# Layer 0 of a four-layer graph kernel: one mask instruction a tile, loads a step earlier, late sums added a step later

## The chip, the core and the metric

The kernel runs on one core of one Trainium2 chip. The time is the device time of one execution in microseconds; for the kernel before, three executions gave 3460.62, 3468.68 and 3473.94 us, so the median is 3468.68 us. The profile is of one more execution, which took 3465.43 us.

The engines are named as in the profile: PE is the matrix engine (PEld its weight loads), DVE the vector engine, ACT the scalar engine, POOL the GpSimd engine, and SP the engine that in this kernel only issues transfers.

## The reference, cut to what matters

There are 64 graphs of 256 nodes with 256 features (`x`), and a weighted adjacency matrix for each (`adj`). Four layers follow each other, each with a residual and a layer norm. The change is in layer 0, a recurrence over the nodes in which node i reads the states of all nodes:

```python
n = h_e.shape[1]
d = jnp.sum(adj, axis=-1)
dinv = jnp.where(d != 0, 1.0 / jnp.where(d != 0, d, 1.0), 0.0)
norm_adjT = jnp.swapaxes(adj, 1, 2) * dinv[:, :, None]

def step(h, i):
    x = jnp.take(h_e, i, axis=1)
    row = jnp.take(norm_adjT, i, axis=1)
    x_par = jnp.einsum('bj,bjd->bd', row, h)
    iou = x @ W_ioux.T + b_ioux + x_par @ W_iouh.T + b_iouh
    r, z = jnp.split(iou, 2, axis=1)
    r, z = (jax.nn.sigmoid(r), jax.nn.sigmoid(z))
    hc = jnp.tanh(x @ W_coux.T + b_coux + x_par * r @ W_couh.T + b_couh)
    h_new = z * x_par + (1.0 - z) * hc
    h = jax.lax.dynamic_update_slice(h, h_new[:, None, :], (0, i, 0))
    return (h, None)
```

At step i the nodes j < i hold new states, and the nodes j >= i still hold their inputs. Layers 1 to 3 (a graph convolution, a masked attention of one head and one of eight) come afterwards and are the same in both kernels.

## The kernel before, in words

**The two halves of the program.** `_recurrence` is layer 0: 256 steps, one after the other, with all 64 graphs in each step. `_layers` then works through layers 1 to 3 graph by graph. In the trace the first step of the recurrence begins at about 138 us and the last one ends at about 1551 us; the rest of the 3463.7 us belongs to the layers.

**A step.** Step n flips `xp` on PE (`xpT_ps`, L614), copies the result on ACT (L616), multiplies it by the gate weights on PE (L607), and takes the sigmoids on ACT (L830 to L835). DVE forms `rx` (L832), PE flips and multiplies it, ACT takes the tanh (L864), and DVE forms `zcc` (L866) and the next `xp` (L869). That last one needs `v` (L855), which needs `ready` (L806): POOL's scaled copy of the sum for the next node. The order on every engine is written out by hand (`manual_schedule`), and an engine that waits holds up all that is behind it.

**Where the sum of a node comes from.** Steps go in 32 parts of 8 (U = 8). In this text, step 13.6 is the one with p = 6 of part 13. `sums[a]` (`ACC`) holds the sums of the eight nodes of part a, and it is filled from five sides.

- The input side, for nodes j >= i: `Us`, made ahead and loaded by `sums_in` (L315). Its first half is made before the recurrence. The second half is made inside it by `x_side` in pieces of four graphs: 16 tiles `xA` and `xX`. Before use, each `xA` must be masked to its lower triangle on POOL by `cut` (L332). A tile needs four pairs of matrix products (L212, called "products" below), and the kernel before masks it in two halves of two graphs each.
- Newest states: DVE adds them one node at a time (`push`, L632).
- States a few steps old: POOL adds two to four nodes at once (`push_far`, L665 and L669). Early in a part it also does the next part's nodes.
- Late side, for states of about the last 64 steps: `late` (L523) runs on PE in steps p = 0 to 3 and reads the ring `Hw`. ACT copies its results, SP sends them to `Lb` in step p = 3 (L503) and receives them as `late_sb` in step p = 4 (L509). POOL adds `late_sb` to the next part's `ACC` in two halves (L878): in the kernel before, nodes 4 to 7 at the end of step p = 5 and nodes 0 to 3 at the end of step p = 6.
- Early side, for older states: `early_fill` (L420) multiplies tiles `Hs` (states, read back from DRAM) and `A`. The results are stored in `Es` (L432), loaded as `early_sb` (L449) and added on POOL (L819).

**What fills the gaps.** In steps p = 4 to 7 there are two places in each step where PE does early work, if its tiles have been begun at least three steps before (`landed`), or otherwise products of `x_side`: one product a place in p = 4 and 5, two in p = 6 and 7.

**The queue of SP.** All transfers of the recurrence are issued by SP in program order. `into_ring` (L658) writes the states into `Hw`, four transfers in each of the steps p = 4 to 7; `late` of the next part reads them. Loads of `x_side`, of the early side, of `raw` and `S` are put in a list by `load_later` and are begun by `next_load` (L268), two in each of the steps p = 0 to 3. Rows of `adj` for the degrees (L300), `xq` (L571) and the stores are issued where they stand. Every transfer on SP also waits until the one that used its semaphore eight transfers before it has landed.

Of the kernel before, what the change touches and what calls it, by code (L numbers as in the profile page):

```python
# [19 lines left out]
P = 128  # L20
# [50 lines left out]
def _recurrence(tc, ident, Hd, x, adj, W_ioux, b_ioux, W_iouh, b_iouh, W_coux, b_coux, W_couh, b_couh, wide, then):  # L71
# [19 lines left out]
    nc = tc.nc  # L91
# [7 lines left out]
    XB = 4  # L99
# [4 lines left out]
    with ExitStack() as ctx:  # L104
# [7 lines left out]
        tri = const.tile([P, P], F32, name="tri")  # L112
# [96 lines left out]
        def x_product(pb, at, A, Xs):  # L209

            for jc, (a, xs) in enumerate(zip(A, Xs)):
                nc.tensor.matmul(  # L212
                    pb[:, at, :], a, xs, start=(jc == 0), stop=(jc == len(A) - 1)
                )

        def x_out(half, b, ub):

            for c in range(2):
                nc.sync.dma_start(
                    Us[c, b:b + 4, half * P:(half + 1) * P, :].rearrange("b i f -> i b f"),  # L220
                    ub[:, :, c * P:(c + 1) * P],
                )
# [22 lines left out]
        def next_of(queue, n):  # L245
            if queue:
                queue.pop(0)(n)

        def next_load(n):
            if loads:  # L250
                loads.pop(0)[1](n)

        def copy_later(out, in_, then=None):
            def f(n):
                nc.scalar.copy(out, in_)
                held.pop(0)
                if then:
                    then(n)

            copies.append(f)  # L260

        def load_later(out, in_, rank):

            begun = []

            def f(n):
                with nc.allow_non_contiguous_dma(reason="bias vector across partitions"):
                    nc.sync.dma_start(out, in_)  # L268
                begun.append(n)

            loads.append((rank, f))
            loads.sort(key=lambda e: e[0])
            return begun

        def landed(begun, n):

            return all(f and n > f[0] + 2 for f in begun)

        def at_step(n, f):
            transfers.setdefault(n, []).append(f)  # L280
# [3 lines left out]
        def base_bank(shape, name):  # L284

            while len(held) == 3:
                next_of(copies, now)
            held.append(name)
            return ps.tile(shape, F32, tag="base", name=name, bufs=3)
# [31 lines left out]
        def x_side():  # L321

            def load(g):
                A = stream.tile([P, XB, P], F32, tag="xA", name=f"xA2_{g}", bufs=3)
                Xs = stream.tile([P, XB, D], F32, tag="xX", name=f"xX2_{g}", bufs=3)
                return A, Xs, [
                    load_later(to, of.rearrange("b j d -> j b d"), 2)
                    for to, of in ((A, adj[g:g + XB, P:N, P:N]), (Xs, x[g:g + XB, P:N, :]))
                ]

            def cut(A, lo):
                nc.gpsimd.tensor_mul(  # L332
                    A[:, lo:lo + 2], A[:, lo:lo + 2], tri.unsqueeze(1).to_broadcast([P, 2, P])
                )

            tiles = [load(e * XB) for e in range(3)]
            ahead = False
            n = yield
            for g in range(0, B, XB):
                A, Xs, last = tiles.pop(0)  # L340
                while not ahead:
                    if landed(last, n):
                        cut(A, 0)
                        ahead = True
                    n = yield
                ub = stream.tile([P, 4, D], F32, tag="ub", name=f"xu2_{g}")
                for b in range(0, XB, 2):
                    pb = base_bank([P, 2, D], f"xp2_{g}_{b}")
                    for q in range(2):
                        x_product(pb, q, [A[:, b + q, :]], [Xs[:, b + q, :]])  # L350
                        if q:
                            copy_later(ub[:, b:b + 2, :], pb, None if b + 2 < XB else (
                                lambda n, b=g, ub=ub: at_step(n + 1, lambda: x_out(1, b, ub))
                            ))
                            if b + 2 < XB:
                                cut(A, b + 2)
                            else:
                                ahead = bool(tiles) and landed(tiles[0][2], n)
                                if ahead:
                                    cut(tiles[0][0], 0)  # L360
                                if g + 3 * XB < B:
                                    tiles.append(load(g + 3 * XB))
                        n = yield
# [309 lines left out]
        sides = {}  # L673
# [8 lines left out]
        with tc.tile_pool(name="r_first_ps", bufs=4, space=bass.MemoryType.PSUM) as xps:  # L682
            for g in range(0, B, GB):
                A, Xs = first_in.pop(0)
# [3 lines left out]
                for n in range(0, GB, 4):  # L688
                    ub = fst.tile([P, 4, D], F32, tag="ub", name=f"xu_{g}_{n}")
                    for e in range(0, 4, 2):  # L690
                        pb = xps.tile([P, 2, D], F32, tag="x", name=f"xp_{g}_{n}_{e}")
                        for q in range(2):
                            b = n + e + q
# [45 lines left out]
        late_side = background = None  # L739
        behind = []  # L740
        x_left = x_side()
        next(x_left)

# [16 lines left out]
        for now in range(N):  # L760
            n = now
            k, i = divmod(n, T)
            p = n % U
# [104 lines left out]
                xp = new("xp", n + 1)  # L868
                nc.vector.scalar_tensor_tensor(xp, zcc, Sd, v, ALU.mult, ALU.add)  # L869
            next_of(copies, n)  # L870
            if p < 4:
                for _ in range(2):
                    next_load(n)

            if p in (5, 6) and n + 8 - p in sides:
                half = slice(0, U // 2) if p == 6 else slice(U // 2, U)
                part = sums[n // U + 1][:, half]
                nc.gpsimd.tensor_add(part, part, sides[n + 8 - p][:, half])  # L878
# [532 lines left out]
def kernel(ctx: ExitStack, tc: tile.TileContext, ins, out):  # L1411
# [14 lines left out]
    def load_layers(load):  # L1426
        weights.extend(
            _load_layers(nc, wide, load, ins["L1_gnn_W"], ins["L1_gnn_b"], l2, l3)
        )

    _recurrence(
        tc, ident, Hd, x, adj,
        *(ins["L0_gnn_" + n] for n in (
# [44 lines left out]
```

## Time and profile before

| | |
|---|---|
| median of three runs | 3468.68 us (3460.62 to 3473.94) |
| profiled execution | 3465.43 us, span of its instructions 3463.7 us |
| granted PE clock, mean over the span | 0.979 |
| busy: PE, PEld, DVE, ACT, POOL | 93%, 67%, 72%, 54%, 54% of the span |
| recurrence, first to last `xpT_ps` | 137.8 to 1549.1 us |
| mask of `xA` on POOL, 128x256 (L332) | 32 times, 725 ns each |
| addition of `late_sb` on POOL, 128x512 (L878) | 60 times, 1268 ns each |
| transfers | 347.89 MB |

Busy shares are means over the recurrence and the layers, which have different limits, so the recurrence is read from its own stretch. A wait is listed as "who waited <- for whom: total us, times, longest us". In the timeline a line is "start us, duration us, engine, line, operation, out<-in"; the brackets at its end tell how long the engine sat idle before it and what ended that. The length of a step is the distance between the starts of two `xpT_ps` flips (L614) in the timeline of PE. In an undisturbed part the eight steps take 5.30, 5.15, 5.15, 5.28, 5.37, 5.14, 4.88 and 4.88 us, together about 41.2 us (part 28, for one).

### The profile page before, as it was taken

What the parts mean: (1) busy time and instruction counts of PE and PEld (TensorE: products, weight loads), DVE (VectorE), ACT (ScalarE), POOL (GpSimd) and SP (SyncE); (2) the same over time, 40 slices, a digit from 0 to 9 for tenths busy, and PEclk for the clock granted to TensorE, in tenths of its full rate; (3) what the DMA queues carried; (4) which work ended last, traced back from release to release, by engine and by line L of the source; (5) the groups of instructions that cost most, each with busy time, mean ns of one, the idle gap of its engine ahead of it and who ended that gap; (6) DMA issues with size and microseconds to landing.
All of it is one profiled execution on the core that took longest, in us unless ns stands there. A gap on an engine that the chain in (4) does not pass through costs nothing.

```text
span 3463.7 us, 80374 instructions
## 1 busy us (share of the span) xinstructions
PE 3228.6 (93%) x29350; PEld 2320.4 (67%) x29350; DVE 2502.0 (72%) x7061; ACT 1883.4 (54%) x5010; POOL 1873.9 (54%) x2181
## 2 busy tenths in 40 slices
PE   5699999999889898887999999999999999999997
PEld 4555555555555555556888888888888888888885
DVE  3366767766666777754888888888888888888875
ACT  0255545444444454444666666666666666666664
POOL 2366677766566777743444444444444444444443
PEclk8999999999999999997999999999999999999999
DMA  9756576687787575321111111111111111111100
GB/s 301 221 153 143 161 173 154 160 187 187 188 208 168 143 175 145 97 64 54 47 47 47 47 47 46 47 47 46 47 47 47 47 47 47 47 47 47 47 28 19
DMA packets 389348, 347.89 MB, mean 100 GB/s; under 512 B 107356, under 2 KB 355304, under 8 KB 383720
## 3 DMA queue, kind: packets, MB, share of 16 engines
q1 hardware_dynamic: 371256, 325.82, 35.0%
q10 hardware_dynamic: 17696, 16.91, 1.5%
q8 instruction: 235, 3.85, 0.5%
q14 instruction: 161, 1.32, 0.1%
HBM read 224.01 MB, written 99.61 MB: 93 GB/s over the span
## 4 chain that ended last, share of the span: by engine, by line
PE 73%; DVE 7%; DMA 7%; POOL 5%; issue 3%; ACT 2%; SPq 2%; ACTq 0%; DVEq 0%; POOLq 0%
PE mm L999 13%; PE rc L607 5%; PE s L1183 4%; PE rc L599 4%; PE mm_2f L999 4%; PE mm_3v L999 3%; PE mm_t L999 3%; PE mm_3f L999 3%; PE mm_2v L999 3%; PE mm_g L999 3%; PE mm_2s L999 3%; DVE ACC L632 3%; PE o L1218 3%; PE mm_2w L999 3%; PE late L523 3%
## 5 line engine op out<-in xcount | busy, mean ns | idle before, releaser
L632 DVE SCALAR_TENSOR_TENSOR ACC<-keep,S,ACC 128x128 f32<-128x128 f32 x1712 | 503.8, 344 | 186.6 <-ACT hs L650 170.7
L1195 POOL TENSOR_TENSOR p3s<-p 128x256 f32<-128x256 f32 x512 | 387.0, 787 | 366.6 <-ACT p L1193 366.2
L999 PE MATMUL mm<-xT,weights 128*128 128x256 f32 x2048 | 481.9, 383 | 2.9 <-ACT xT L1081 2.9
L999 PEld LDWEIGHTS mm<-xT,weights 128*128 128x128 f32 x2048 | 384.8, 190 | 79.5 <-issue 25.5
L1192 DVE TENSOR_TENSOR p<-s,neg 128x512 f32<-128x512 f32 x512 | 317.5, 682 | 114.5 <-PE s L1183 114.5
L669 POOL TENSOR_TENSOR ACC<-ACC,far 128x384 f32<-128x384 f32 (+1 forms) x313 | 372.3, 1189 | 24.5
L599 PE MATMUL rc<-WxT,xqT 128*64 128x256 f32 x2048 | 326.6, 397 | 4.0 <-ACT rc L840 1.2
L665 POOL TENSOR_TENSOR far<-hs,S 128x384 f32<-128x384 f32 (+1 forms) x313 | 304.3, 972 | 4.7
L963 ACT ACTIVATE y<-y,shift,rstd 128x256 f32<-128x256 f32 x512 | 273.4, 599 | 48.6 <-DVE shift L961 44.7
L806 POOL TENSOR_TENSOR ready<-ACC,dinv 128x128 f32<-128x128 f32 x255 | 101.9, 400 | 364.3 <-DVE ACC L632 363.8
L1193 ACT ACTIVATE p<-p 128x512 f32<-128x512 f32 x512 | 295.0, 628 | 2.1 <-DVE p L1192 1.6
L1106 ACT ACTIVATE qk<-mm,weights 128x256 f32<-128x256 f32 x256 | 107.5, 471 | 268.0 <-PE mm L999 268.0
L1095 POOL TENSOR_TENSOR y<-y,g 128x512 f32<-128x512 f32 x64 | 81.0, 1265 | 267.4 <-issue 267.4
L1232 DVE RECIPROCAL rT<-o 128x256 f32<-128x256 f32 x128 | 223.7, 1748 | 0.2 <-PE o L1209 0.2
L955 POOL TENSOR_TENSOR rstd<-rstd,mhalf 128x2 f32<-128x2 f32 x256 | 173.6, 696 | 84.2 <-DVE rstd L954 82.4
L951 DVE BATCH_NORM_STATS2 st<-y 128x6 f32<-128x256 f32 x512 | 208.8, 408 | 13.4 <-POOL y L1095 12.6
L616 ACT COPY xpT<-xpT_ps 128x128 f32<-128x128 f32 x256 | 68.4, 267 | 265.6 <-PE xpT_ps L614 265.6
L607 PE MATMUL rc<-WhT,xpT 128*64 128x128 f32 x2048 | 170.5, 288 | 28.2 <-ACT xpT L616 28.0
L1060 POOL TENSOR_TENSOR dis<-dis,mhalf 128x2 f32<-128x2 f32 x64 | 44.8, 700 | 277.0 <-DVE dis L1059 252.1
L607 PEld LDWEIGHTS rc<-WhT,xpT 128*64 128x64 f32 x2048 | 107.9, 137 | 118.4 <-ACT xpT L616 84.0
L212 PE MATMUL xp<-xX,xA 128*128 128x256 f32 x384 | 109.4, 423 | 66.3 <-POOL xA L685 39.5
L1158 ACT ACTIVATE qk<-mm,weights 128x256 f32<-128x256 f32 x256 | 107.5, 471 | 115.9 <-PE mm L999 115.9
(162 smaller groups left out, 7485.1 us busy)
## 6 DMA issues: line engine op xcount, KB each, us to landing
xX<-in_x_dram ACTq DMA_DIRECT2D x16, 1024.0 KB
Us<-xu SPq DMA_DIRECT2D x64, 256.0 KB
xq<-in_x_dram SPq DMA_DIRECT2D x64, 256.0 KB
ACC<-Us SPq DMA_DIRECT2D x32, 512.0 KB
Es<-eu SPq DMA_DIRECT2D x64, 256.0 KB
early_sb<-Es SPq DMA_DIRECT2D x32, 512.0 KB
xin<-in_x_dram SPq DMA_DIRECT2D x64, 256.0 KB
ad<-in_adj_dram SPq DMA_DIRECT2D x64, 256.0 KB
```

The costliest lines, as they stand in the source:

```text
L599: nc.tensor.matmul(G[o * B:(o + 1) * B], xqT[a, i // 2][:, i % 2, kc, h * B:(h + 1) * B], WxT[:, kc, o, gates], start=False, stop=False, s ...
L607: nc.tensor.matmul(G[o * B:(o + 1) * B], hT[:, kc * B:(kc + 1) * B], WhT[:, kc, o, g], start=False, stop=(kc == 1), skip_group_check=True,)
L632: nc.vector.scalar_tensor_tensor(acc[:, 0, :], keep[:, j % 2, :], s, acc[:, 0, :], ALU.mult, ALU.add)
L665: nc.gpsimd.tensor_mul(tmp[:, 0:count, :], hs.unsqueeze(1).to_broadcast(shape), s.unsqueeze(2).to_broadcast(shape),)
L669: nc.gpsimd.tensor_add(acc, acc, tmp[:, 0:count, :])
L951: nc.vector.bn_stats(st, y[:, c, :])
L963: nc.scalar.activation(y[:, c, :], y[:, c, :], AF.Identity, bias=shift[:, c:c + 1], scale=rstd[:, c:c + 1],)
L999: nc.tensor.matmul(pm[:, c, :], lhsT[:, k, c * P:(c + 1) * P], rhs[:, k, :], start=(k == 0), stop=(k == 1),)
L1192: nc.vector.tensor_add(p, s_ps[i], self.neg3)
L1193: nc.scalar.activation(p, p, AF.Exp, scale=ISQ)
L1195: nc.gpsimd.tensor_add(both, p[:, 0, :], p[:, 1, :])
L1232: nc.vector.reciprocal(rT, o_ps[:, 1, :])
```

## The change

It makes three edits. The mask of an `xA` tile becomes one POOL instruction over all four graphs (128x512) instead of two over two graphs each. It is still issued when the tile before is finished, or, where the tile's transfers had not been begun three steps before, at the next place. The list of loads is worked off two at a time in steps p = 7, 0, 1 and 2 instead of 0, 1, 2 and 3. The two halves of `late_sb` are added at the end of steps p = 6 (nodes 0 to 3, as before) and p = 7 (nodes 4 to 7, before: p = 5).

```diff
-            def cut(A, lo):
-                nc.gpsimd.tensor_mul(
-                    A[:, lo:lo + 2], A[:, lo:lo + 2], tri.unsqueeze(1).to_broadcast([P, 2, P])
-                )
+            def cut(A):
+                nc.gpsimd.tensor_mul(A, A, tri.unsqueeze(1).to_broadcast([P, XB, P]))
...
                     if landed(last, n):
-                        cut(A, 0)
+                        cut(A)
                         ahead = True
...
-                            if b + 2 < XB:
-                                cut(A, b + 2)
-                            else:
+                            if b + 2 == XB:
                                 ahead = bool(tiles) and landed(tiles[0][2], n)
                                 if ahead:
-                                    cut(tiles[0][0], 0)
+                                    cut(tiles[0][0])
...
-            if p < 4:
+            if p in (7, 0, 1, 2):
                 for _ in range(2):
                     next_load(n)

-            if p in (5, 6) and n + 8 - p in sides:
+            if p in (6, 7) and n + 8 - p in sides:
                 half = slice(0, U // 2) if p == 6 else slice(U // 2, U)
                 part = sums[n // U + 1][:, half]
                 nc.gpsimd.tensor_add(part, part, sides[n + 8 - p][:, half])
```

## The prediction

> **What bounds the kernel now.** I read the lengths of the 256 steps first, from the starts of the `xpT_ps` flips. The 255 distances sum to 1411 us; 31 undisturbed parts of 41.2 us and seven steps of 4.88 would take 1311. So about 100 us are stalls, nearly all in steps p = 6 and 7 of two groups of parts: 30 us in parts 0 to 9 and about 38 us in parts 13 to 19. The lists of waits of POOL and of PE, over 137 to 1551 us, name both:
>
> ```profile
> POOL ready L806 <- DVE ACC L632: 363.8, 201, 6.8
> POOL ACC L878 <- DMA late_sb<-Lb: 44.5, 10, 9.2
> ```
>
> ```profile
> PE xp L212 <- POOL xA L332: 16.8, 15, 2.4
> PE late L523 <- DMA Hw<-hs: 3.5, 1, 3.5
> ```
>
> The first group is PE waiting for a mask. The timelines of POOL and then of PE show it in steps 1.6 and 1.7 (starts 214.06 and 221.37):
>
> ```profile
> 213.34 1.27 POOL L878 TENSOR_TENSOR ACC<-ACC,late_sb 128x512 f32<-128x512 f32 x1
> 214.57 0.72 POOL L332 TENSOR_TENSOR xA<-xA,tri 128x256 f32<-128x256 f32 x1
> 215.38 0.40 POOL L806 TENSOR_TENSOR ready<-ACC,dinv 128x128 f32<-128x128 f32 x1
> 215.74 0.83 POOL L665 TENSOR_TENSOR far<-hs,S 128x384 f32<-128x384 f32 x1
> 216.64 1.00 POOL L669 TENSOR_TENSOR ACC<-ACC,far 128x384 f32<-128x384 f32 x1
> 217.59 0.73 POOL L332 TENSOR_TENSOR xA<-xA,tri 128x256 f32<-128x256 f32 x1
> ```
>
> ```profile
> 218.38 0.70 PE L212 MATMUL xp<-xX,xA 128*128 128x256 f32 x2 [0.68 <-POOL xA L332]
> 218.91 0.27 PE L614 MATMUL rT_ps<-ident,rx 128*128 128x128 f32 x1
> ```
>
> The mask at 217.59 was asked for at the second place of the step. POOL had `ready` and two `push_far` instructions in front, and the flip of `rx` stood behind the waiting product. The flip came 4.85 us into the step instead of 2.4 (step 20.6), and the step took 7.31 us for 4.92. At p = 7, where POOL has four nodes to add instead of three, the same costs 2.97.
>
> The second group is the late side. POOL waits at the end of p = 5 up to 9.2 us for `late_sb`, with `ready` behind it and so the next `xp`. Why it is late, the timeline of SP tells (part 16, steps 1 to 7):
>
> ```profile
> 863.46 12.61 SPq L268 DMA_DIRECT2D Hs<-Hd  x1
> ...
> 878.83 5.36 SPq L268 DMA_DIRECT2D raw<-in_adj_dram  x1
> 884.29 2.11 SPq L503 DMA_DIRECT2D Lb<-lb  x2
> 886.50 2.27 SPq L658 DMA_DIRECT2D Hw<-hs  x4
> 888.94 0.34 SPq L509 DMA_DIRECT2D late_sb<-Lb  x1
> 889.32 6.52 SPq L658 DMA_DIRECT2D Hw<-hs  x8
> 895.95 1.34 SPq L432 DMA_DIRECT2D Es<-eu  x2
> 897.38 3.05 SPq L658 DMA_DIRECT2D Hw<-hs  x4
> 900.54 0.60 SPq L268 DMA_DIRECT2D Hs<-Hd  x1
> ```
>
> Here SP has hardly a gap from one round to the next. The send, programmed for p = 3, goes out in p = 5. In parts 12, 13, 15, 16, 17 and 19 SP almost never waits for a state: one round, from the last `Hw` write to the next, takes 42.8, 46.0, 49.5, 48.2, 49.5 and 49.1 us. In those parts SP and the transfers set the period, and the late wait is where the compute side notices.
>
> **What the Trainium skill says.** "Perfetto Trace Analysis", What "DMA-bound" means, counts as one kind an issuing sequencer whose track is solid transfers; the trace agrees above. "DMA: Bandwidth & Descriptors", Issuing engines are not separate DMA queues, says that all transfers end on the same 16 engines; in this trace their busy share is near 1.0 in steps p = 0 to 4 of parts 13 to 19, and 0.3 to 0.6 in p = 6 and 7. "GPSIMD Engine Reference", Elementwise, gives some 2.6 cycles an element for two inputs; I use the trace's own durations.
>
> **The mask.** Thirty-two masks of 725 ns (23.2 us of POOL) become sixteen. The 128x1024 one (L685) takes 2342 ns, so by a straight line 512 columns take 725 + 256 x 2.105 = 1264 ns, as L878 does with 1268: 20.3 us. The 3 us of POOL are worth nothing by themselves, since it waits 364 us for DVE. What counts is position. The mask in the middle of a tile goes, and with it the wait there. The mask at a tile's end stays, is 0.54 us longer, and the next product follows at once. From the instruction orders of both kernels I took, for each step, where a tile ends.
>
> - A tile ends at the second place (3.6, 3.7, 7.6): the mask is again behind `ready` and `push_far`, so 2.39 + 0.54 = 2.93 at p = 6 (twice) and 2.97 + 0.54 = 3.51 at p = 7 (once). Sum 9.4.
> - A tile ends at the first place (1.6, 2.6, 6.6, 10.6, 1.7, 6.7): `push_far` ends 4.42 us into p = 5. In 1.6 the mask ends 0.55 into the step, and the product is wanted at 0.60: nothing. With an `An` mask (735 ns) in between it is 0.7 late, of which the gates' slack of 0.2 hides some: 0.5 each, three times. At 1.7 the first-half addition is in front, which ends 4.81 into p = 6: 0.45. At 6.7 `An` is too: 0.8. Sum 2.8.
>
> Before, the mask stalls were 2.39, 5.36, 3.32, 2.98, 2.77, 7.80, 2.98 and 2.77 us in parts 0, 1, 2, 3, 5, 6, 7 and 9: 30.4. After: 12.2. **Gain 18.2 us.** It reaches the end if SP doesn't bind in these parts: it still waits for states there, mostly 2 to 8 us a part. Bounds: 22 if first-place waits hide, 10 if SP takes some.
>
> **The late addition.** Sixty instructions remain sixty. At p = 5 the end of the step gets free; at p = 7 POOL ends `push_far` 4.08 us into the step, so the addition at 5.35, that is 0.47 into p = 0, and an `An` mask behind it at 1.2. The `ready` of p = 0 is due at 1.3 to 1.45, and DVE's pushes to nodes 4 and 5 come later: nothing added. The wait for `late_sb` gets a step, 5.1 us, more. Of the waits of 4.26, 9.19, 6.67, 7.56, 2.69 and 8.86 us in parts 13 and 15 to 19, only 8 to 10 us of stall would be left, of some 38.
>
> **The loads.** This is where I doubt the rest. SP runs ahead of the steps: in the list above the first `Hs` load is issued right after the last `Hw` write of p = 7 although it is programmed for p = 0. Between that write and the send at p = 3 lie the same eight loads, before and after; only their order against `Es`, `early_sb` and `xq` changes. The round of SP therefore stays as long, some 48 us in parts 15 to 19 against 41.2 of compute, and the stall moves. **What is late next** is `Hw` at p = 0: `late` (L523) is wanted 1.76 us into that step, and the last `Hw` write landed 4.5 to 5.7 us after its issue where PE waited for it (17.0, 18.0, 14.0). With part 15's p = 6 and 7 undisturbed, `late` would be wanted 4 us before that. All that is gained is the slack at the end of the group (20.0: 6.75 us after the last write, 4.7 needed), 2 us, and some 2 us where SP waited for states or ACT in its round: **4 us**. Bounds: -3 (`rows` for the degrees come behind two more loads and keep DVE waiting at p = 2) and 30 (the round gets shorter).
>
> Early tiles move too: one of part 11 moves to part 21 and one of part 23 to part 25, at 0.6 us of PE a place, in gaps. The last `Us` stores move from part 9 to part 10 and 11, where SP has some 2 us spare: nothing. The sum is 18.2 + 4 = 22 us: 3465.4 - 22 = 3443 for the profiled execution, and 3468.7 - 22 = 3446 against the median, which stands 3.3 above it.
>
> **The rivals.**
> - The late wait goes and nothing takes its place: 18 + 30 = 48 us, 3420. For it: ten waits, 44.5 us. Against it: SP's rounds without a gap. Chance 0.14.
> - SP takes the mask's gain too: parts 3, 7 and 8 leave it under 3 us of waiting a part, so a shorter compute makes it the bound, and 5 to 15 us remain: 3458. Chance 0.21.
> - Slower: SP's round gets longer in parts 12 to 19, as two `Hs` loads stand in front of the `Es` stores that `early_sb` waits for, and the send comes later. From 4.4 us a round (35 us over eight) it outweighs the gain and the bound below; at 5 us it is 40 - 18 = 22 slower, 3491. Against it: the same bytes in the same queue. Chance 0.05.
> - The loads are in effect not a step earlier: that is part of my forecast.
>
> **How the numbers follow.** My forecast (3446, alone 3437 to 3456) has 0.60. A measurement of this kernel tells about 0.5% from no change, 17.3 us, or 3451.3. Faster: the first rival's 0.14, some 0.5 of the forecast and 0.03 of the second, 0.67. Same: 0.28. Slower: 0.05. The range goes from 3422, near the first rival, to 3463, past the second.
>
> **What would show it.** Right: 16 masks of about 1264 ns; stalls of 2.9, 3.5 and 2.9 us in 3.6, 3.7 and 7.6 and none in 1.6, 5.6 and 9.6; no `late_sb` wait at p = 5; PE waiting for `Hw` at p = 0 in parts 14 to 20, with SP's rounds still near 48 us. Wrong: rounds under 44 us there (the first rival), over 52 (the slower one), or parts 0 to 9 no shorter.

## The result: 2.55% slower

The changed kernel takes 3556.01 us (median of four executions, 3551.38 to 3563.34), the kernel before 3468.22 us beside it. The ratio is 1.0255, with a 95% interval of 1.0240 to 1.0269. The forecast of 3446 us, and its range of 3422 to 3463, had the wrong sign.

In the profiled execution the span is 3555.6 us. Between the first and the last `xpT_ps` lie 1502.5 us, against 1411.3 before: 91.1 us more, so the whole loss lies in the recurrence: 28.4 us of it in parts 0 to 9, the rest behind them. By the place p of the step within its part, summed over the parts, the difference is +55.7 at p = 0, +7.7 at p = 3, +26.9 at p = 4, -28.9 at p = 6 and +31.7 at p = 7, and under 2 us at the others. So p = 6, the place at which the change aimed, did get shorter, and p = 0, 4 and 7 got longer.

(Lines of `_recurrence` after the mask stand four lower than before: L878 is now L874, L806 is L802, L523 is L519, L503 is L499, L658 is L654. L268, the loads, keeps its number.)

**The mask, answered.** The list of waits of PE over the recurrence and the timelines of POOL and PE in step 3.6 of the changed kernel (start 303.43) show this step as forecast:

```profile
PE xp L212 <- POOL xA L332: 7.8, 6, 2.6
```

```profile
304.75 0.40 POOL L802 TENSOR_TENSOR ready<-ACC,dinv 128x128 f32<-128x128 f32 x1 [2.12 <-DVE ACC L628]
305.11 0.83 POOL L661 TENSOR_TENSOR far<-hs,S 128x384 f32<-128x384 f32 x1
306.02 0.99 POOL L665 TENSOR_TENSOR ACC<-ACC,far 128x384 f32<-128x384 f32 x1
306.97 1.27 POOL L332 TENSOR_TENSOR xA<-xA,tri 128x512 f32<-128x512 f32 x1
```

```profile
308.29 0.70 PE L212 MATMUL xp<-xX,xA 128*128 128x256 f32 x2 [2.00 <-POOL xA L332]
```

PE's wait for masks fell from 16.8 us to 7.8. The mask of 512 columns took 1.27 us, and step 3.6 was 2.93 us too long, exactly its term in the prediction. The other terms for masks came out larger (below, "Why the prediction was wrong").

**The queue of SP, answered.** This is the timeline of SP over part 17 (steps 17.0 to 17.7, from 959.96 us). A line is "start, duration, engine, line, transfer":

```profile
955.00 4.88 SPq L654 DMA_DIRECT2D Hw<-hs  x8
959.92 1.07 SPq L268 DMA_DIRECT2D Hs<-Hd  x2
961.04 1.26 SPq L428 DMA_DIRECT2D Es<-eu  x2
962.39 4.20 SPq L268 DMA_DIRECT2D A<-in_adj_dram  x1
966.63 5.49 SPq L268 DMA_DIRECT2D Hs<-Hd  x1
972.16 0.43 SPq L445 DMA_DIRECT2D early_sb<-Es  x1
972.69 1.18 SPq L300 DMA_DIRECT2D rows<-in_adj_dram  x2
973.97 0.54 SPq L268 DMA_DIRECT2D Hs<-Hd  x1
990.31 0.33 SPq L268 DMA_DIRECT2D A<-in_adj_dram  x1
990.73 0.73 SPq L315 DMA_DIRECT2D ACC<-Us  x1
991.51 0.96 SPq L268 DMA_DIRECT2D raw<-in_adj_dram  x2
992.51 3.55 SPq L567 DMA_DIRECT2D xq<-in_x_dram  x2
996.16 1.33 SPq L499 DMA_DIRECT2D Lb<-lb  x2
...
1002.14 0.35 SPq L505 DMA_DIRECT2D late_sb<-Lb  x1
```

Between 974.51 and 990.31 SP issues nothing: 15.8 us in which the whole queue stands behind one load, the second `A` of the part. Two windows of the same stretch (the columns after the length are busy time and count of PE, PEld, DVE, ACT and POOL, the granted clock, the share of the transfer engines, and GB/s) show what that does to the transfers, which had been the busy resource:

```profile
974.60:982.00 7.40, 7.20 (x120) 4.05 (x115) 4.48 (x16) 3.22 (x11) 4.29 (x5) 1.00 1.02 279
982.00:990.20 8.20, 5.66 (x78) 2.95 (x76) 7.01 (x24) 4.27 (x16) 4.80 (x6) 1.00 0.16 42
```

For 8 us the share is 0.16: the loads issued earlier have drained, and nothing new is asked for. What ends the gap stands in the timeline of PE: the second half of the early tile at p = 4 of part 17 (step start 987.76).

```profile
989.61 0.64 PE L416 MATMUL early<-Hs,A 112*32 112x256 f32 x8
990.26 0.33 PE L610 MATMUL rT_ps<-ident,rx 128*128 128x128 f32 x1
```

The waits of SP in the kernel before, and then in the changed kernel, put a size on it (the releaser is the next thing that PE did, the flip of `rx`):

```profile
SPq L268 <- PE rT_ps L614: 2.5, 10, 0.4
SPq L268 <- PE early L420: 1.0, 2, 0.5
```

```profile
SPq L268 <- PE rT_ps L610: 160.1, 13, 23.1
SPq L268 <- PE early L416: 31.4, 2, 16.7
```

From 3.5 us of waiting for PE (2.5 and 1.0 for `early`) the loads went to 191.5 us. SP stands still before a load of `A` at p = 4 of parts 4, 8, 12 to 18, 20 and 24, for 15 to 23 us each, and for 5 in part 15.

**What is late behind the gap.** The send at L499 goes out at p = 5, `late_sb` lands in p = 7, and even the addition that was moved to p = 6 and 7 waits for it. The timeline of POOL in 17.7 and of PE in 18.0 tells the two costs of this gap:

```profile
1005.66 1.26 POOL L874 TENSOR_TENSOR ACC<-ACC,late_sb 128x512 f32<-128x512 f32 x1 [3.67 <-DMA late_sb<-Lb]
```

```profile
1019.43 1.10 PE L519 MATMUL late<-Hw,An 64*32 64x256 f32 x32 [2.03 <-DMA Hw<-hs]
```

Step 17.7 took 10.79 us for 4.88, and 18.0 took 10.30 for 5.30: part 17's `Hw` writes stand in the queue behind the late send. In parts 14 and 18 it is the `rows` for the degrees that come late, and DVE, which has all pushes behind it, waits (14.4 is 14.5 us too long, 18.4 is 13.1). The waits of DVE and of ACT over the recurrence:

```profile
DVE ACC L628 <- POOL ACC L874: 35.0, 9, 5.3
DVE deg L303 <- DMA rows<-in_adj_dram: 28.4, 5, 11.9
```

```profile
ACT xu L255 <- DMA Us<-xu: 17.3, 4, 7.4
ACT eu L255 <- DMA Es<-eu: 12.2, 9, 3.6
```

The last two lines are a second, smaller loss; the lists before have no such wait for `Us` or `Es`. At p = 7 two loads now stand in SP's queue ahead of the stores of that step. ACT may write a `ub` buffer again only when its store has landed, and it waits: 7.6 us too long in step 7.7, 4.9 in 2.0, 6.5 in 7.0.

**Why the second `A` has no buffer.** `A` serves two early tiles, an even one t and t + 1, and its pool has two buffers. A load into the third `A` waits until PE has used tile t + 1 of the first. Early pieces may be begun at steps 25, 57, 89 and so on, which is p = 1 of parts 3, 7, 11 and so on; `early_ahead` then queues one tile a step, and `next_load` begins it in the next step. Before, loads were begun at p = 2 and p = 3, two tiles in part 3, so every part used its pairs (0, 1), (2, 3) whole. With p = 3 taken off the list, one tile is loaded there. The order of the instructions shows one early tile in parts 3, 7, 11 and 23 where before had two, and three for two in parts 5, 9, 21 and 25. From then on each part uses an odd tile at p = 4, then an even, an odd, an even. The `A` of that odd tile is still held when the part's second `A` is to be loaded at p = 0 or 1. The profile counts the same: PE's `early` products in parts 3, 7, 11 and 23 fall from 32 to 16, and those in parts 5, 9, 21 and 25 rise from 32 to 48. That the loads wait is in the trace; that this parity is the cause is what the experiments test.

### The profile page after: what moved, and what is told of

Its sections match the earlier page's. It is cut to its first block, busy times and chain, and to the rows that moved or that the text cites. A ratio compares the mean times of both kernels' runs of the same rounds, so it can differ in the third digit from the quotient of the medians.

```text
span 3555.6 us, 80310 instructions
## 1 busy us (share of the span) xinstructions
PE 3255.8 (92%) x29350; PEld 2339.4 (66%) x29350; DVE 2503.5 (70%) x7061; ACT 1883.5 (53%) x5010; POOL 1874.9 (53%) x2165
## 4 chain that ended last, share of the span: by engine, by line
PE 69%; DMA 8%; POOL 7%; DVE 7%; issue 5%; ACT 2%; SPq 2%; ACTq 0%; DVEq 0%; POOLq 0%
PE mm L995 13%; PE rc L603 4%; PE s L1179 4%; PE rc L595 3%; PE mm_2f L995 3%; PE mm_3v L995 3%; PE mm_t L995 3%; PE mm_3f L995 3%; PE mm_2v L995 3%; PE mm_g L995 3%; PE mm_2s L995 3%; PE o L1214 3%; PE mm_2w L995 3%; DVE ACC L628 3%; POOL ACC L665 3%
## 5 line engine op out<-in xcount | busy, mean ns | idle before, releaser
L802 POOL TENSOR_TENSOR ready<-ACC,dinv 128x128 f32<-128x128 f32 x255 | 102.3, 401 | 465.1 <-DVE ACC L628 462.1
L595 PE MATMUL rc<-WxT,xqT 128*64 128x256 f32 x2048 | 341.8, 413 | 5.2 <-issue 1.6
L1102 ACT ACTIVATE qk<-mm,weights 128x256 f32<-128x256 f32 x256 | 107.5, 471 | 269.6 <-PE mm L995 269.6
L947 DVE BATCH_NORM_STATS2 st<-y 128x6 f32<-128x256 f32 x512 | 209.0, 408 | 10.6 <-POOL y L1091 9.8
L862 DVE TENSOR_TENSOR zcc<-zc,rc 128x128 f32<-128x128 f32 x256 | 72.8, 284 | 183.2 <-ACT rc L860 182.7
L519 PE MATMUL late<-Hw,An 64*32 64x256 f32 x3840 | 159.4, 401 | 32.2 <-DMA Hw<-hs 17.3
```

The costliest lines, as they stand in the source:

```text
L595: nc.tensor.matmul(G[o * B:(o + 1) * B], xqT[a, i // 2][:, i % 2, kc, h * B:(h + 1) * B], WxT[:, kc, o, gates], start=False, stop=False, s ...
L947: nc.vector.bn_stats(st, y[:, c, :])
```

## The experiments

The two theories: **held buffer** (a load waits on SP for an `A` that PE uses at p = 4) against **longer round** (two loads at p = 7 and more of them ahead of the stores lengthen SP's round; stores behind loads stall ACT). All ratios are against the kernel before on the same chip, whose medians there were 3465.8 to 3468.2 us.

### Each edit alone, and two without the third

Each of these kernels is the kernel before with the named hunks of the diff in "The change", and nothing else.

The mask edit alone:

> The kernel before with the mask edit alone (one 128x512 mask a tile ahead; loads and late addition where they were). Theory, the queue of transfers: the whole loss comes from the moved loads, and the mask edit does what its steps said, so about 18 us less than before, 3450. Rival, the mask itself costs (a long mask on POOL delays ready): 3475 or more.

Measured: 3466.64 us, ratio 1.0006 (0.9996 to 1.0016). Neither case: nothing gained. The timelines of POOL and PE in step 5.6 (start 388.86) say why:

```profile
390.53 0.83 POOL L661 TENSOR_TENSOR far<-hs,S 128x384 f32<-128x384 f32 x1
391.44 0.99 POOL L665 TENSOR_TENSOR ACC<-ACC,far 128x384 f32<-128x384 f32 x1
392.39 1.26 POOL L332 TENSOR_TENSOR xA<-xA,tri 128x512 f32<-128x512 f32 x1
```

```profile
393.70 1.22 PE L212 MATMUL xp<-xX,xA 128*128 128x256 f32 x2 [2.00 <-POOL xA L332]
```

In the loads' old order a tile ends at the second place of steps 3.7, 5.6, 7.7 and 9.6. There the mask stands behind `push_far` as the half did, and is longer: these steps are 4.4 to 5.0 us too long. In 1.6, 2.6 and 6.6 a tile ends at the first place, but POOL has the addition of p = 5 (and in two of them an `An` mask) ahead of the mask: 2.0, 2.7 and 4.2 us. In the changed kernel 5.6 and 9.6 do early work, and p = 5 has no addition. So the mask edit needs the loads moved, so that tiles end in other steps, and the addition away from p = 5.

The moved loads alone:

> The kernel before with the moved loads alone (last and first three places of a part; masks in halves, late addition at p=5 and p=6). Theory, the queue of transfers: with a load into A at p=0 or p=1 held on SP until PE has used an early tile at p=4, the send slips to p=5, in about ten parts; the addition, still at p=5, then waits longer than in the changed kernel. So the changed kernel's loss of about 88 us, plus the 18 us of mask that are not gained, plus up to 40 us of late addition: 3575 to 3620. Rival, the later addition at p=7 is the cause: within 15 us of before.

Measured: 3553.17 us, ratio 1.0249 (1.0234 to 1.0265). The loads alone make the whole loss; the rival is out. The time is 22 us under the expected range, and its interval overlaps the changed kernel's, so the other two edits gained nothing on top. The waits of POOL say why:

```profile
POOL ACC L878 <- DMA late_sb<-Lb: 84.4, 12, 9.2
```

The addition, still at p = 5 and 6, takes the wait, and with it `Hw` at the next p = 0 is in time (p = 0 sums to 178.7 us, as before). In the changed kernel the same gap is paid in two shares, at p = 7 and at the next p = 0.

The late addition alone:

> The kernel before with the late addition alone at p=6 and p=7. Theory, the queue of transfers: the send goes out at p=3 as before, the wait of POOL for late_sb has one step more, and the wait moves in part to Hw at the next p=0: 5 to 30 us less than before, 3440 to 3464. Rival, the addition at p=7 stands in the way of the next part's first ready: 3490 or more.

Measured: 3465.81 us, ratio 1.0006 (0.9994 to 1.0017), just above the expected range. In its profile the steps with p = 6 and 7 are 31.4 us shorter than before and those with p = 0 are 22.8 longer; the recurrence is 3.5 us shorter, but that execution took 3459.7 us, and the median shows no gain. Most of the wait for `late_sb` (44.5 us before, 7.8 now) has become a wait for `Hw` (3.5 and 18.9). An addition at p = 7 costs nothing that can be seen.

Mask and late addition, without the moved loads:

> The kernel before with the mask edit and the late addition, loads begun at p=0 to p=3 as before: the changed kernel without its moved loads. Theory, the queue of transfers: the two gains add, 3425 to 3448, so the moved loads alone cost the changed kernel some 110 to 130 us. Rival, the three edits are bad only together (SP's round is lengthened by the mask's tiles that come free later): 3480 or more.

Measured: 3460.19 us, ratio 0.9979 (0.9971 to 0.9986). The two together gain 0.2%, less than expected; the moved loads then cost the changed kernel some 96 us (3556 - 3460).

### Taking the held buffer away, in two ways

Each piece may be begun one step sooner, so that parts 3, 7, 11 and 23 load two tiles again:

```diff
-                (25, 2, 0, 16), (57, 3, 0, 48), (89, 4, 0, 80), (121, 5, 0, 112), (89, 6, 0, 80),
-                (153, 6, 80, 144), (121, 7, 0, 112), (185, 7, 112, 176),
+                (24, 2, 0, 16), (56, 3, 0, 48), (88, 4, 0, 80), (120, 5, 0, 112), (88, 6, 0, 80),
+                (152, 6, 80, 144), (120, 7, 0, 112), (184, 7, 112, 176),
```

> The changed kernel, and each early piece may be loaded one step sooner (the eight numbers 25, 57, 89, ... in the list of pieces are one less). In parts 3, 11 and 23 two early tiles are then loaded where the changed kernel has one, so that the even tile, whose load takes a new A, is used at p=4 as before. Nothing else is moved. Theory, a load held on SP for an A buffer that PE uses at p=4: the held loads go (no gap of SP over 6 us before a load of A in parts 12 to 20, against 15 to 23 us), the send is back at p=3, and most of the loss goes: 3430 to 3475. Rival, the moved loads stand ahead of the stores at p=7 and ScalarE waits for ub: 3530 or more. Rival, more or larger transfers a round make SP's round long: 3540 or more.

Measured: 3450.43 us, ratio 0.9956 (0.9941 to 0.9972): 106 us less than the changed kernel, with the loads still at p = 7, 0, 1 and 2. In the list of SP's waits the loads' wait for that flip of PE has shrunk to 2.0 us, and in the timeline of SP over its part 17 (from 889.4 us) the queue moves on, and the send goes out at p = 3:

```profile
SPq L268 <- PE rT_ps L610: 2.0, 9, 0.3
```

```profile
899.35 0.53 SPq L268 DMA_DIRECT2D A<-in_adj_dram  x1
900.17 6.64 SPq L268 DMA_DIRECT2D Hs<-Hd  x1
906.91 0.90 SPq L315 DMA_DIRECT2D ACC<-Us  x1
907.86 1.05 SPq L268 DMA_DIRECT2D raw<-in_adj_dram  x2
908.95 5.14 SPq L567 DMA_DIRECT2D xq<-in_x_dram  x2
914.24 1.33 SPq L499 DMA_DIRECT2D Lb<-lb  x2
```

The other way leaves the order of tiles alone and gives each early tile its own `A` of half the size, in four buffers, which is the same memory:

```diff
-            if t % 2 == 0:
-                A = stream.tile([P, 2 * GB, T], F32, tag="A", name=f"A_{k}_{lo}_{t}")
-                last.append(load_later(
-                    A[0:rows],
-                    adj[t * GB:(t + 2) * GB, lo:hi, k * T:(k + 1) * T].rearrange("b j i -> j b i"), 1
-                ))
-                got[:] = [A]
-            early_in.append((last, k, lo, hi, t, Hs, *got))
+            A = stream.tile([P, GB, T], F32, tag="A", name=f"A_{k}_{lo}_{t}", bufs=4)
+            last.append(load_later(
+                A[0:rows],
+                adj[t * GB:(t + 1) * GB, lo:hi, k * T:(k + 1) * T].rearrange("b j i -> j b i"), 1
+            ))
+            early_in.append((last, k, lo, hi, t, Hs, A))
```

> The changed kernel with one A of half the size for each early tile, in four buffers in place of two: the same memory, the same bytes, two loads a tile in place of three for two tiles; the order of tiles is the changed kernel's. A buffer then comes free with each tile. Theory, a load held for an A buffer: the held loads go although the odd tile stays at p=4, and the time is 3430 to 3490. Rival, the order of the tiles itself or the round's length is the cause: 3530 or more; four more loads a part would make it longer still.

Measured: 3454.86 us, ratio 0.9966 (0.9955 to 0.9977). Its odd tile stays at p = 4, and its list of SP's waits has

```profile
SPq L268 <- PE rT_ps L608: 9.1, 3, 3.9
```

No load of `A` is held there for more than 3 us. Two mends that share only this, that no load waits long for a buffer of `A`, each take away 101 us or more. The small tiles have a price of their own: steps 14.5 and 18.5 are 9.2 and 10.9 us too long, as POOL waits there for `raw`.

### Putting the held buffer into the kernel before

None of the three edits; only the eight step numbers, one later (26, 58, 90, ...):

> The kernel before, none of the three edits, with one thing changed: each early piece may be loaded one step later (the eight numbers 25, 57, 89, ... are one more). Parts 3, 11 and 23 then load one early tile where before loads two, so the odd tile is used at p=4, as in the changed kernel. Theory, a load held for an A buffer: the same loads are held although no load is moved, the send slips past p=4, and the time is near that of the moved loads alone: 3530 to 3580. Rival, it needs the loads at p=7 (longer round, stores behind them): within 20 us of before.

Measured: 3547.83 us, ratio 1.0225 (1.0212 to 1.0238). The waits of SP:

```profile
SPq L268 <- PE rT_ps L614: 173.6, 14, 26.2
```

The loss comes back with no load at p = 7 and no edit of the change. So the parity of the early tiles, and with it the held buffer, is enough by itself; loads at p = 7 aren't needed for the loss.

### The stores behind the loads

The two loads of p = 7 are issued behind that step's transfers:

```diff
-            if p in (7, 0, 1, 2):
+            if p in (0, 1, 2):
                 for _ in range(2):
                     next_load(n)
...
             for f in transfers.pop(n, ()):
                 f()
+            if p == 7:
+                for _ in range(2):
+                    next_load(n)
```

> The changed kernel, with the two loads of p=7 issued behind the stores and transfers of that step, not ahead of them. Theory, ScalarE's waits for ub come from stores that stand behind loads, and are the small part of the loss: 15 to 35 us less than the changed kernel, 3520 to 3540; the held loads of A and the late sends stay. Rival, ub is the main cause: under 3490.

Measured: 3530.88 us, ratio 1.0181 (1.0161 to 1.0201): 25 us less than the changed kernel, and the wait of ACT for `Us` stores fell from 17.3 to 4.9 us. That is the small part, as expected. Other waits of ACT grew (for `hs` behind `Hw` and `Hs` transfers from 15.6 to 37.2 us), so the 25 us are the net of both.

> Both mends in the changed kernel: pieces one step sooner, and the two loads of p=7 behind the stores. Theory, a held A buffer and stores behind loads are the whole of the loss: 3415 to 3445, at or under the kernel before with mask and late edits alone. Rival, the loads at p=7 lengthen SP's round by themselves: 3455 or more.

Measured: 3445.63 us, ratio 0.9935 (0.9917 to 0.9952). This is the fastest kernel of the study, 0.65% faster than the kernel before. Of the 25 us only some 5 are left to gain once no buffer is held, and the two intervals overlap, so that share isn't settled. A reason that the order of the copies suggests, and that wasn't tried by itself, so it isn't shown: a `ub` also holds two early tiles, so a part with one early tile leaves a half-filled `ub` until the next part, and ACT has one buffer in place of two.

### What each edit is worth once the buffer is free

Both are the changed kernel with the pieces one step sooner (0.9956), less one edit.

> The changed kernel with the pieces one step sooner, and with the late addition put back to p=5 and p=6. The prediction's step: the late addition is worth its waits for late_sb at p=6, less what moves to Hw; as the late edit alone gave nothing, the time is that of the changed kernel with the pieces one step sooner, 3447 to 3457. Rival, the addition is worth its 20 us or so once Hw has room: 3465 or more.

Measured: 3464.45 us, ratio 0.9990 (0.9981 to 0.9999). The late edit is worth 0.34% here, 12 to 14 us, near the rival. POOL's wait for `late_sb` is 17.8 us without it and 4.7 with it.

> The changed kernel with the pieces one step sooner, and with the masks in halves again (a half a tile ahead, a half after the first bank). The prediction's step: with the loads moved the mask edit is worth 18 us, 3464 to 3472. Rival, with the loads moved tiles have landed so early that halves do as well: 3447 to 3457.

Measured: 3461.91 us, ratio 0.9978 (0.9969 to 0.9988): the mask edit is worth 0.22%, 8 to 11 us, between the two cases. Without it the steps with p = 6 and 7 are 18.5 us longer in the profile, and those with p = 0 are 9.3 us shorter. Where half of the gain is given back, the traces show: with the mask edit steps 2.0, 7.0 and 8.0 are 4.7, 5.4 and 5.7 us too long, without it 0.4, 1.2 and 0.2. In them ACT waits for the `Us` store behind the loads of p = 7. Its list of waits, with the mask edit and then without it, has

```profile
ACT xu L255 <- DMA Us<-xu: 13.6, 3, 4.9
```

```profile
ACT xu L255 <- DMA Us<-xu: 6.0, 3, 2.1
```

The steps come sooner with the edit, but the stores not by as much: step 8.0 starts 13.0 us sooner, the store before it is issued 9.1 sooner.

> Three mends in the changed kernel: pieces one step sooner, one half-size A a tile in four buffers, and the two loads of p=7 behind the stores. If held loads are gone already with the pieces one step sooner, smaller A tiles add nothing, or cost their eight more loads a round of four tiles at most: 3440 to 3455. If loads are still held for A somewhere, 3425 to 3440.

Measured: 3454.72 us, ratio 0.9954 (0.9938 to 0.9970). Smaller `A` tiles add nothing more, as no load is held any longer; the median is even 9 us above that of the same kernel without them (3445.63 us), though the two intervals overlap. Here too POOL waits for its transfers in 14.5 and 18.5 (9.8 and 12.1 us too long).

## Why the prediction was wrong

**The step that failed** is in "The loads": "Between that write and the send at p = 3 lie the same eight loads, before and after; only their order changes", and after it "one of part 11 moves to part 21 and one of part 23 to part 25, at 0.6 us of PE a place, in gaps". The loads were counted right, and so was their number of bytes. What was not asked of a moved load is whether its **destination** is free when its turn comes. The sentence on the early tiles had the cause in hand, an odd number of tiles, and priced it as PE time. It was worth 101 to 106 us (the two mends), not nothing. It was also incomplete: one tile of part 3 moved to part 5 and one of part 7 to part 9, and the held loads of parts 4 and 8 come from these.

**The size of SP's round.** Forecast: still near 48 us. Measured from the last `Hw` write to the next, in parts 12 to 19: 51.2, 52.2, 58.4, 46.4, 54.5, 55.1, 56.8 and 49.4 us, together 424.0 against 378.3 before. That is 5.7 us more a round, 46 in all. The slower rival had this place, this sign and about this size ("from 4.4 us a round"), with another mechanism; it was given 0.05 because of "the same bytes in the same queue". Bytes don't decide where a queue stands still. The prediction's own sign for that case, rounds over 52 us, appeared in five of the eight. But its 3491 us is 65 short. It left out parts 0 to 9, for one: they took 476.3 us against 447.9, and "parts 0 to 9 no shorter" was the prediction's other sign of being wrong.

**The stalls before** were read too narrowly: by the same undisturbed lengths, steps p = 6 and 7 hold some 74 of the 100 us, and not nearly all.

**The bound of -3 for `rows`** failed with the same step: DVE waited 28.4 us for `rows`, since they stand behind the held load.

**The stores.** The prediction saw that the loads' order against `Es` and the other stores changes, but not that ACT's next write to `ub` waits for a store: up to 25 us (3556.0 - 3530.9).

**The mask.** In the changed kernel 3.6 cost 2.93 as worked out, 3.7 cost 5.05 for 3.51, 7.6 cost 4.16 for 2.93, and 5.6 and 9.6 nothing. The two terms that were too small leave out that PE's clock falls after a stall (last section). The tiles that end at the first place cost 6.3 us for 2.8: 0.7 in 1.6, where PE waited for no mask, 1.3 each in 2.6, 6.6 and 10.6, 0.7 in 1.7 and 0.9 in 6.7. These steps sum to 18.4 us for the 12.2 that were worked out, so the edit took away some 12 us of stalls in the changed kernel, not 18.2. With no buffer held, tiles end in other steps, and the 18.5 us of p = 6 and 7 there are near the forecast without confirming its sum. Of these 8 to 11 us reach the end: the second rival, SP taking the mask's gain, was right about the half that is lost, but by way of stores that ACT waits for at p = 0, which it did not name. Without the loads moved, the edit gave nothing.

**The late addition** cost nothing, and what came next was `Hw` at p = 0, as forecast. The late edit alone left nothing in the median (3465.81 us, ratio 1.0006) where the prediction had 4 us. With the loads early and no buffer held it was worth 12 to 14 us, so here moving the loads did make room, which the prediction denied.

With the buffer free, the change is worth 15 us (3450.43 us), and with the stores first 20 us; the forecast had 22. The totals are close, but part of that is luck: the mask brought less and the late addition more than in the sum.

The Trainium skill has the symptom: "Perfetto Trace Analysis", Optimization Strategy under Identifying Performance Opportunities, says that a gap repeating on the engine that should be saturated can mean that there is not enough SBUF for the next tile (buffer count, tile sizes). The trace agrees, though here the gap is on the queue and not on a compute engine: SP stood for 15 to 23 us in ten parts, and no longer with four half-size buffers in the same memory.

## What to carry to other kernels

When a load is moved earlier in an in-order queue, look up for each moved load who last used its buffer and when, and compare the two times; one load that must wait holds every transfer behind it, however free their own buffers are. When a tile is shared by two users, a shift by one user changes which of them ends a round, so check the parity of the whole chain and not only the first tile moved. Where two loops work at one rate, price the moved work by its waits and not by its own time: here 0.6 us of PE at another place was worth 100 us.

## What the runs showed of the hardware that was not expected

A stall of PE can be paid twice. These are windows of the changed kernel in and after steps 3.6 and 3.7 (the number after the five busy times is the granted clock); the last one lies within the third:

```profile
303.40:311.20 7.80, 5.80 (x54) 3.68 (x52) 3.57 (x12) 2.95 (x10) 4.62 (x5) 1.00 0.12 37
311.20:316.00 4.80, 2.93 (x27) 1.89 (x23) 2.37 (x8) 1.43 (x6) 3.25 (x4) 1.00 0.40 77
316.00:321.20 5.20, 4.51 (x29) 2.76 (x29) 0.93 (x3) 1.53 (x4) 1.86 (x2) 0.67 0.46 124
317.54:320.95 3.41, 3.41 (x24) 2.12 (x26) 0.93 (x3) 1.53 (x4) 0.32 (x1) 0.50 0.21 62
```

PE waited 2.00 us for the mask in 3.6 and kept its clock. In 3.7 it waited 2.56 us, and the next 5.2 us had a mean clock of 0.67; after the `Hw` wait of 18.0 it is 0.67 too, over 5.1 us. The length of the wait alone doesn't decide: in 7.6 a wait of 2.00 us, as in 3.6, was followed by 0.68 over 4.2 us. The Trainium skill, "TensorE: Matmul & The Clock Gate", What's actually happening, tells of a clock halved after an idle window of some 3.4 us, and of full speed again after some 3.4 us of sustained work. The way back agrees: the last window is 3.41 us at half clock, with PE busy throughout. That the clock fell after 2.0 and 2.6 us of waiting, in steps in which PE had other short gaps, is earlier than the page says. Over the whole recurrence the mean clock was 0.98 before and 0.96 in the changed kernel.

An idle stretch of the queue is made up only in part: while SP stood, the share of the transfer engines fell to 0.16 (42 GB/s, against 279 just before), and in parts 12 to 19, where SP stood some 107 us before loads of `A`, the eight rounds grew by 46. And a small store behind other transfers frees its buffer late: in step 7.7 the `Us` store was issued at 511.14 us behind two `Hs` loads, and ACT could go on writing only at 519.05, 7.9 us later.
